# Cross-attention with layer norm on one core: when the next weights are turned, and which engine turns the later context

## The chip, the cores and the metric

The kernel runs on one core of a Trainium2 chip. A core has five engines that run side by side, each with its own queue of instructions: TensorE (matrix products and transposes), VectorE, ScalarE, GpSimd and SyncE, which here only issues DMA transfers. In the profile they are called PE (with PEld for the loading of weights), DVE, ACT, POOL and SP. An engine executes its queue in order, and an instruction waits until what it needs has been signalled by another engine or by a DMA that has landed. The metric is the device time of one execution in microseconds (us).

## What is computed

There are 16 batches of 256 queries of width 256, and 16 contexts of 77 keys of width 192. With 8 heads of width 256 the reference is, in short:

```python
Q = (img_embed @ Wq).reshape(B, -1, H, D).transpose(0, 2, 1, 3)
K = (sent_embed @ Wk).reshape(B, -1, H, D).transpose(0, 2, 1, 3)
V = (sent_embed @ Wv).reshape(B, -1, H, D).transpose(0, 2, 1, 3)
score = jnp.einsum('bhqd,bhkd->bhqk', Q, K) / math.sqrt(D)
mask = (atten_mask != 0)[:, None, None, :]
score = jnp.where(mask, score, -jnp.inf)
attn = jax.nn.softmax(score, axis=-1)
ctx = jnp.einsum('bhqk,bhkd->bqhd', attn, V).reshape(B, -1, H * D)
out = ctx @ Wo + img_embed
mu = jnp.mean(out, axis=-1, keepdims=True)
var = jnp.var(out, axis=-1, keepdims=True)
return (out - mu) * jax.lax.rsqrt(var + EPS) * gamma + beta
```

All values are 32-bit floats.

## The kernel before

The kernel never forms Q, K and V. For each head it multiplies the weights first: G = Wk Wq^T / 16 for the scores and U = Wv Wo for the output. Then A = G context^T (called `pa` in PSUM, `a` in SBUF) stands for a batch's keys, and the scores of a tile of 128 queries are x^T against A. The order of every engine's instructions is written out by hand: the kernel runs under a manual schedule, so the queues hold what the Python code issues, in that order.

The context width of 192 is split into 128 rows (`cA`) and 64 rows (`cB`; these are stored twice, in both halves of the partitions, so that two products can run side by side). G and U are split in the same way into `gA`, `gB` and `uA`, `uB`. The 77 keys are split into 64 and 13; the last 13 keys of all batches are gathered in `cRA` and `cRB`, and their product with U is `pr`, formed once by `prepare_last`.

The setup stage (until about 58 us of the profile) runs like this:

- SyncE issues the loads: the rows of Wk and Wq for the first head pairs (`wk_nat`, `wk_last`, `wq_nat`, L567 to L571), the first 336 rows of the context (`c_sb`, L564), then Wk and Wq for the other heads in blocks of 32 rows (`wk_blk`, `wq_blk`, L561), the other 896 rows of the context (`c_sb` again), Wv in blocks (`wvT`), Wo (`wo`, L590), the mask (`bias`, L591) and x in blocks (`xT`, L168). Later follow x in rows (`xg`, L144), gamma and beta. Each transfer counts on one of eight semaphores in turn, and it is issued only after the eighth transfer before it has landed.
- TensorE transposes the first weights through PSUM (`turn_k`, `turn_q`, L615; an identity matrix is the other operand), and ScalarE and VectorE in turn copy the results out (`evacuate`, L151 and L153). TensorE forms `pg` (L719, copied to `gA` by ScalarE, L726) and `ph` (L733, to `gB` by VectorE, L740). Then `turn_c(0, first)` transposes the first context rows on TensorE (`pc`, L653), with copies to `cA` and `cB` and a GpSimd copy of `cB` into the other half (L664).
- `a_of_places((0, 1))` forms the first half of A for the first group of four batches: 64 products with `cA` (`pa`, L199), 64 with `cB` (L213), and eight copies. The weights in blocks need no TensorE: `turn_blk` (L642) has VectorE transpose them in blocks of 32x32, and the following products (`pgb` L676, `phb` L690) contract over the blocks. `turn_blk(0)` stands before this call, `turn_blk(1)` among its copies, after the fourth.
- After `pgb` and `phb`, VectorE turns `wvT` (`turn_v`, L668), the second half of A is formed, and `turn_c(first, NCR)` transposes the remaining eight chunks of 112 context rows: 16 transposes on TensorE, four copies each on ScalarE, VectorE and GpSimd. GpSimd then gathers `cRA` and `cRB` (L782, L783), clears `vr` (L784) and turns the mask into a bias (L788).
- TensorE forms U (`pu` L676, then `pw` L690). ScalarE and VectorE copy it to `uA` and `uB`, and GpSimd copies `uB` to the other half (L807). `pr` follows (L274 with `cRA` and `uA`, L284 with `cRB` and `uB`), then the main loop.

The main loop runs over the 16 batches: scores (`ps`, L313), bias and maximum on VectorE (L328, L335), exponential on ScalarE (L342), normalising on GpSimd (L356), the turn of the weights on VectorE (L366), the products with the values (L429, L378), and the layer norm. PSUM has eight banks, from which all these results are taken in turn.

Of the kernel before, what the change touches and what calls it, by code (L numbers as in the profile page):

```python
# [8 lines left out]
F32 = mybir.dt.float32  # L9
# [6 lines left out]
P = 128  # L16
H = 8
D = 256
EPS = 1e-05
GB = 4  # L20
KM = 64
# [32 lines left out]
def kernel(  # L54
# [13 lines left out]
    nc = tc.nc  # L68
    B, S, DI = x.shape
    S2, DL = c.shape[1], c.shape[2]  # L70
    LB = DL - P
    CR = 112
    NCR = B * S2 // CR
    NG = B // GB
    QT = S // P
    NT = B * QT
# [3 lines left out]
    BK = 32  # L80
    NM = P // BK
    NL = DL // BK
    PW = (NF + 1) * BK
    assert KM == 2 * BK and NM == NF and 2 * KR <= BK
    assert NCR * CR == B * S2 and NG * GB == B and DI == 2 * P and D == 2 * P and 2 * LB == P


    engines = mybir.EngineType
# [25 lines left out]
    def of_e(u, e):  # L114
        return u[:, 3 - 2 * e : 5 - 2 * e].rearrange("p q n i c -> p (q n) i c")


    cA = const.tile([P, B, S2], F32, tag="cA", name="cA")
    cB = const.tile([P, B, S2], F32, tag="cB", name="cB")
    cRA = const.tile([P, B, KR], F32, tag="cRA", name="cRA")  # L120
    cRB = const.tile([P, B, KR], F32, tag="cRB", name="cRB")
# [12 lines left out]
    c_rows = c.rearrange("b k l -> (b k) l").rearrange("(r p) l -> p r l", p=CR)  # L134

    def flat(ap):
        return ap.rearrange("p a b -> p (a b)")
# [10 lines left out]
    def evacuate(dst, src):  # L148
        evacs[0] += 1
        if evacs[0] % 2:  # L150
            nc.scalar.copy(dst, src)  # L151
        else:
            nc.vector.tensor_copy(dst, src)  # L153
# [386 lines left out]
    early = ctx.enter_context(tc.tile_pool(name="early", bufs=1))  # L540
    pools[0] = turned = early
    with tc.tile_pool(name="wonce", bufs=1) as wp:
        c_sb = wp.tile([CR, NCR, DL], F32, tag="c", name="c_sb")


        wq_nat = wp.tile([P, 2, 2, 2 * D], F32, tag="w128", name="wq_nat")
# [12 lines left out]
        def load_blocks(to, blocks):  # L559
            for i in range(NM):  # L560
                nc.sync.dma_start(to[i * BK : (i + 1) * BK], blocks[i])  # L561

        def load_c(lo, hi):
            nc.sync.dma_start(c_sb[:, lo:hi, :], c_rows[:, lo:hi, :])  # L564

        first = -(-GB * S2 // CR)
        nc.sync.dma_start(wk_nat[:, 0], wk_rows[0][:, : 2 * D])  # L567
        nc.sync.dma_start(wk_last, wk_ends[:, : 2 * D])
        nc.sync.dma_start(wq_nat[:, 0], wq_rows[0][:, :, : 2 * D])
        nc.sync.dma_start(wk_nat[:, 1], wk_rows[1][:, : 2 * D])  # L570
        nc.sync.dma_start(wq_nat[:, 1], wq_rows[1][:, :, : 2 * D])  # L571
        load_c(0, first)
        for e in range(2):
            load_blocks(wk_blk[:, e], wk_blocks[2 * e + 1])
            load_blocks(wq_blk[:, e], wq_blocks[2 * e + 1])
        load_c(first, NCR)

        warm = const.tile([P, 1], F32, tag="warm", name="warm")
        nc.scalar.activation(warm, eps, AF.Exp)
# [8 lines left out]
            load_blocks(wvT[:, a], wv_blocks[a])  # L588
        for a in range(NF):
            nc.sync.dma_start(wo_of[a // 2][:, a % 2], wo_rows[a])  # L590
        nc.sync.dma_start(  # L591
            bias_f.bitcast(I32), mask.rearrange("b k -> (b k)").partition_broadcast(P)
        )
# [17 lines left out]
        def turn_chunks(of, name):  # L611

            pt = ps_mm.tile([P, 4, P], F32, tag="mm", name=f"pt_{name}")
            for i, chunk in enumerate(of):
                nc.tensor.transpose(pt[:, i], chunk, ident)  # L615
            return pt

        def turn_q(e, u):
            chunks = [
                wq_nat[:, e, t, u * D + dc * P : u * D + (dc + 1) * P]  # L620
                for dc in range(2) for t in range(2)
            ]
            pt = turn_chunks(chunks, f"q_{e}_{u}")
            evacuate(flat(qT[:, e, u]), flat(pt))

        def turn_k(e):
            pt = turn_chunks([wk_nat[:, e, n * P : (n + 1) * P] for n in range(4)], f"k_{e}")
            evacuate(
                kT[:, e].rearrange("p u n l -> p (u n) l")[:, :, :P], pt
            )  # L630
# [9 lines left out]
        def turn_blk(e):  # L640
            for blk, of in ((wk_blk, kT_blk), (wq_blk, qT_blk)):
                nc.vector.transpose(  # L642
                    of[:, e].rearrange("p n (m r) -> p m n r", r=BK),
                    blk[:, e].rearrange("p m (n c) -> p m n c", c=BK),
                )

        def turn_c(lo, hi):
            for r in range(lo, hi, 2):
                n = min(2, hi - r)
                pc = ps_mm.tile([P, 4, P], F32, tag="mm", name=f"pc_{r}")  # L650
                for lc in range(2):
                    for j in range(n):
                        nc.tensor.transpose(  # L653
                            pc[:, 2 * lc + j, :CR],
                            c_sb[:, r + j, lc * LB : lc * LB + P],
                            ident[:CR, :CR],
                        )
                rows = slice(r * CR, (r + n) * CR)
                evacuate(flat(cA)[:, rows].rearrange("p (j m) -> p j m", m=CR), pc[:, :n, :CR])
                evacuate(  # L660
                    flat(cB)[LB:, rows].rearrange("p (j m) -> p j m", m=CR),
                    pc[LB:, 2 : 2 + n, :CR],
                )
                nc.gpsimd.tensor_copy(flat(cB)[:LB, rows], flat(cB)[LB:, rows])  # L664

        def turn_v(a):
            blocks = wvT[:, a].rearrange("p m (c n) -> p m n c", n=4)
            nc.vector.transpose(blocks, blocks)  # L668
# [3 lines left out]
        def of_pair(out, a, weight, moving):  # L672

            for n in range(4):
                for e in range(2):
                    nc.tensor.matmul(  # L676
                        out[e][:, a % 2, :],
                        weight(a, e, n)[:, :P],
                        moving(a, e, n),
                        start=(n == 0),  # L680
                        stop=(n == 3),
                    )
# [16 lines left out]
        def two_banks(name, j):  # L699
            return [ps_mm.tile([P, 2, DI], F32, tag="mm", name=f"{name}_{j}_{e}") for e in range(2)]  # L700
# [13 lines left out]
        def g_of(e):  # L714

            pg = ps_mm.tile([P, 2, DI], F32, tag="mm", name=f"pg_{e}")
            for u in range(2):
                for dc in range(2):
                    nc.tensor.matmul(  # L719
                        pg[:, u],  # L720
                        kT[:, e, u, dc, :P],
                        qT[:, e, u, dc],
                        start=(dc == 0),
                        stop=(dc == 1),
                    )
            nc.scalar.mul(gA[:, NF * e : NF * e + 2], pg, D ** -0.5)  # L726

        def rest_of_g(u):

            ph = ps_mm.tile([P, DI], F32, tag="mm", name=f"ph_{u}")  # L730
            for dc in range(2):
                for e in range(2):
                    nc.tensor.matmul(  # L733
                        ph[half(e)],
                        kT[:, e, u, dc, P:],
                        qT[:, e, u, dc],
                        start=(dc == 0),
                        stop=(dc == 1),
                    )
            nc.vector.tensor_scalar(gB[:, u], ph, D ** -0.5, None, ALU.mult)  # L740

        def a_of_places(places, between=None):
            part_A, part_B, copies = prepare_a(0, places)
            part_A()
            part_B()
            for i, (dst, src) in enumerate(copies()):
                evacuate(dst, src)
                if between and i == 3:
                    between()

        turn_k(0)
        keep_busy(2)
# [1 line left out]
        keep_busy(3)  # L754
        turn_q(0, 0)
        turn_q(0, 1)
        g_of(0)
        turn_k(1)
        turn_q(1, 0)
        turn_q(1, 1)  # L760
        g_of(1)
        rest_of_g(0)
        rest_of_g(1)
        turn_c(0, first)
        turn_blk(0)
        a_of_places((0, 1), lambda: turn_blk(1))
        pg = two_banks("pgb", 0)
        for e in range(2):
            of_pair(pg, e, wk_part, wq_part)
# [8 lines left out]
        nc.sync.dma_start(bet, beta.partition_broadcast(P))  # L778
        a_of_places((2, 3))
        turn_v(3)  # L780
        turn_c(first, NCR)
        nc.gpsimd.tensor_copy(cRA, cA[:, :, KM:])  # L782
        nc.gpsimd.tensor_copy(cRB, cB[:, :, KM:])  # L783
        nc.gpsimd.memset(vr, 0.0)  # L784


# [3 lines left out]
        for j in range(NF // 2):  # L790
            pu = two_banks("pu", j)
            for a in range(2 * j, 2 * j + 2):
                of_pair(pu, a, wv_part, wo_part)
            for e in range(2):
                evacuate(
                    of_e(uA, e)[:, :, 2 * j : 2 * j + 2].rearrange("p n a c -> p a n c"),
                    pu[e].rearrange("p a (n c) -> p a n c", c=BK),
                )
# [32 lines left out]
    for b in range(-1, B - 1):  # L831
# [9 lines left out]
        g, n = (b + 1) // GB + 1, (b + 1) % GB  # L841
# [107 lines left out]
```

## Time and profile before

| what | value |
|---|---|
| time, median of 3 runs | 283.19 us (283.01 to 283.97) |
| the profiled execution, its own time | 282.59 us |
| its span, first to last instruction | 280.8 us |
| mean granted TensorE clock | 0.991 |
| TensorE busy | 270.8 us (96%) |
| VectorE busy | 206.1 us (73%) |
| GpSimd busy | 168.2 us (60%) |
| ScalarE busy | 166.5 us (59%) |

The page of the profile gives busy times in 40 equal slices of about 7 us, in tenths:

```profile
PE   7899999999999999999999999999999999999990
DVE  0255762668748989888889787777797978788873
ACT  2312142148547767676767676767686866968751
POOL 1000049955677777786867878777778445426173
DMA  6998898940000010960100109501001011010112
```

The first eight slices are the setup. There the DMA engines are busy almost throughout, and afterwards they are mostly idle. In the views below, a line of a timeline or of the chain starts with the start and the duration in us, then engine, line of code and instruction. Matmul ends are modelled, so the starts of the next instruction are the safer numbers. Times are compared with times of executions, spans with spans; what lies between (1.8 us here) is outside the first and last instruction.

### The profile page before, as it was taken

Reading aid. Unit: us, or ns where it says so; the run is one execution under the profiler, and the core shown is the slowest. Engines: PE = TensorE matmul, PEld = TensorE weight load, DVE = VectorE, ACT = ScalarE, POOL = GpSimd, SP = SyncE. Lnnn points to the kernel's source line nnn. Section 1 sums busy time; section 2 is a strip of 40 time slices with the busy share of each in tenths; the row PEclk is TensorE's granted clock in tenths of the full one; section 3 lists DMA queues with packets and bytes.
Section 4 is the critical chain, followed back from the end, with each engine's and each line's share of the span. In section 5 each row is a group of like instructions: output and inputs, shape, how many; then the busy total and the mean of one; then the engine's idle time right before and its main releaser. Section 6 shows DMA issues by size and latency. Waiting matters only on the chain.

```text
span 280.8 us, 13274 instructions
## 1 busy us (share of the span) xinstructions
PE 270.8 (96%) x5925; PEld 195.6 (70%) x5925; DVE 206.1 (73%) x421; ACT 166.5 (59%) x447; POOL 168.2 (60%) x228
## 2 busy tenths in 40 slices
PE   7899999999999999999999999999999999999990
PEld 7756589985586868686868686868686868476550
DVE  0255762668748989888889787777797978788873
ACT  2312142148547767676767676767686866968751
POOL 1000049955677777786867878777778445426173
PEclk9999999999999999999999999999999999999996
DMA  6998898940000010960100109501001011010112
GB/s 191 246 230 176 279 267 227 166 139 4 2 6 2 5 40 2 191 189 5 42 3 5 40 5 198 180 8 38 7 2 42 2 42 38 4 41 2 40 37 78
DMA packets 35641, 22.61 MB, mean 81 GB/s; under 512 B 17712, under 2 KB 34048, under 8 KB 35584
## 3 DMA queue, kind: packets, MB, share of 16 engines
q1 hardware_dynamic: 35584, 21.77, 30.8%
q8 instruction: 46, 0.75, 1.2%
q14 instruction: 11, 0.09, 0.1%
HBM read 17.57 MB, written 4.19 MB: 77 GB/s over the span
## 4 chain that ended last, share of the span: by engine, by line
PE 89%; POOL 2%; ACT 2%; DMA 2%; DVE 2%; issue 0%; SPq 0%; ACTq 0%; POOLq 0%
PE ps L313 23%; PE pa L199 12%; PE pv L241 9%; PE po L429 9%; PE pm L429 7%; PE pa L213 6%; PE pv L252 5%; PE po L378 5%; PE pu L676 3%; PE pr L274 2%; DMA wq_nat<-in_L_xattn_Wq_dram 2%; ACT e L342 1%; PE pg L719 1%; PE pgb L676 1%; PE pw L690 1%; PE pr L284 1%
## 5 line engine op out<-in xcount | busy, mean ns | idle before, releaser
L342 ACT ACTIVATE e<-s,top 128x77 f32<-128x77 f32 x256 | 67.1, 346 | 52.1 <-DVE top L335 49.9
L356 POOL TENSOR_TENSOR p<-e,rden 128x512 f32<-128x512 f32 x64 | 45.8, 738 | 46.6 <-DVE rden L350 46.4
L313 PE MATMUL ps<-a,xT 128*32 128x154 f32 x2048 | 70.0, 294 | 0.0
L313 PEld LDWEIGHTS ps<-a,xT 128*32 128x32 f32 x2048 | 66.2, 110 | 1.6 <-issue 0.7
L328 DVE TENSOR_TENSOR s<-ps,bias 128x308 f32<-128x308 f32 x64 | 30.3, 475 | 17.6 <-PE ps L313 15.9
L199 PE MATMUL pa<-cA,gA 128*32 128x308 f32 x512 | 35.8, 423 | 0.4 <-ACT cA L151 0.4
L462 POOL TENSOR_TENSOR xg<-xg,m 128x256 f32<-128x256 f32 x33 | 24.2, 733 | 13.5 <-DVE xg L476 11.8
L199 PEld LDWEIGHTS pa<-cA,gA 128*32 128x32 f32 x512 | 16.4, 110 | 21.1 <-issue 7.6
L241 PE MATMUL pv<-uA,cA 128*32 128x512 f32 x256 | 30.4, 592 | 0.0
L366 DVE STREAM_TRANSPOSE pT<-p 128x640 f32<-128x640 f32 x32 | 25.6, 824 | 2.4 <-POOL p L356 2.4
L348 DVE TENSOR_REDUCE den<-e 128x8 f32<-128x616 f32 x32 | 24.7, 772 | 3.5 <-ACT e L342 3.5
L335 DVE TENSOR_REDUCE top<-s 128x8 f32<-128x616 f32 x32 | 25.4, 795 | 1.1
L664 POOL COPY cB<-cB 64x224 f32<-64x224 f32 (+1 forms) x6 | 1.9, 358 | 36.8 <-DVE cB L153 36.8
L392 POOL TENSOR_TENSOR ts<-vw 128x768 f32<-128x768 f32 x11 | 22.0, 1997 | 0.0
L213 PE MATMUL pa<-cB,gB 64*32 64x308 f32 x512 | 19.5, 420 | 0.0
L378 PE MATMUL po<-vw,pT 128*32 128x256 f32 x320 | 19.2, 380 | 0.0
L861 ACT COPY vw<-pv 128x512 f32<-128x512 f32 x32 | 16.9, 578 | 2.5 <-PE pv L252 2.5
L495 ACT ACT_TABLE_LOAD x14 | 18.0, 1283 | 0.3
L213 PEld LDWEIGHTS pa<-cB,gB 64*32 64x32 f32 x512 | 9.7, 107 | 11.3 <-issue 7.6
L252 PE MATMUL pv<-uB,cB 64*32 64x512 f32 x256 | 17.4, 601 | 0.0
L524 DVE SCALAR_TENSOR_TENSOR xg<-xg,mv,gam 128x256 f32<-128x256 f32 x25 | 17.1, 682 | 0.0
L861 ACT COPY a<-pa 128x308 f32<-128x308 f32 x48 | 16.6, 446 | 0.0
(114 smaller groups left out, 440.1 us busy)
## 6 DMA issues: line engine op xcount, KB each, us to landing
xT<-in_x_dram SPq DMA_DIRECT2D x16, 256.0 KB, 6.4
xg<-in_x_dram SPq DMA_DIRECT2D x4, 1024.0 KB, 8.0
out_dram<-xg SPq DMA_DIRECT2D x15, 256.0 KB, 2.3
wo<-in_L_xattn_Wo_dram SPq DMA_DIRECT2D x4, 512.0 KB, 5.3
wvT<-in_L_xattn_Wv_dram SPq DMA_DIRECT2D x16, 96.0 KB, 3.7
wq_nat<-in_L_xattn_Wq_dram SPq DMA_DIRECT2D x2, 512.0 KB, 6.7
wq_blk<-in_L_xattn_Wq_dram SPq DMA_DIRECT2D x8, 128.0 KB, 4.3
wk_blk<-in_L_xattn_Wk_dram SPq DMA_DIRECT2D x8, 96.0 KB, 6.1
```

Of the source, the lines that this page charges most:

```text
L199: nc.tensor.matmul(flat(o[i * BK : (i + 1) * BK]), gA[:, h, cols(dc, i)], flat(cA[:, batches, :]), start=not B_first, stop=B_first,)
L213: nc.tensor.matmul(flat(banks[j + k][i * BK : (i + 1) * BK]), gB[half(k), h % NF, cols(dc, i)], flat(cB[half(k), batches, :]), start=B_fir ...
L241: nc.tensor.matmul(pv[k][i * BK : (i + 1) * BK], cA[:, b, k * BK : (k + 1) * BK], uA[:, parts, :, i], start=True, stop=False,)
L252: nc.tensor.matmul(pv[k][i * BK : (i + 1) * BK], cB[half(k), b, k * BK : (k + 1) * BK], uB[half(k), parts, :, i], start=False, stop=True,)
L313: nc.tensor.matmul(ps[m // 2][i * BK : (i + 1) * BK, m % 2 * 2 * S2 : (m % 2 + 1) * 2 * S2], xT_of[g][:, j * NM + m, dc], flat(a_of[g][:, ...
L328: nc.vector.tensor_tensor(s[:, a * H // 2 : (a + 1) * H // 2], ps[a][:, : H // 2 * S2].rearrange("p (h k) -> p h k", k=S2), bias[:, b, :]. ...
L342: nc.scalar.activation(e[:, h], s[:, h], AF.Exp, bias=top[:, h : h + 1])
L356: nc.gpsimd.tensor_tensor(part, e_mh[:, :, :, keys], rden_mh.unsqueeze(3).to_broadcast(list(part.shape)), ALU.mult,)
L366: nc.vector.transpose(pT_of[t].rearrange("p n m q -> p m n q"), p.rearrange("p m (n k) -> p m n k", k=BK),)
L378: nc.tensor.matmul(po[i * BK : (i + 1) * BK], pT[:, n, i], vw_of[b][:, 2 - n // 2 * 2 : 4 - n // 2 * 2, n % 2, :] if n < NF else vr[:, b, ...
L429: nc.tensor.matmul(out[i * BK : (i + 1) * BK], weight[:, i], moving, start=(n == 0), stop=(n == len(terms) - 1),)
L861: nc.scalar.copy(dst, src)
```

## The change

Four things change.

First, the order of the setup on TensorE: `turn_k(1)` goes ahead of `g_of(0)`, and `turn_c` (for the first context rows) ahead of `g_of(1)`. Second, `turn_blk(1)` goes ahead of `a_of_places((0, 1))` instead of between its copies. Third, the context rows beyond the first 336 are no longer loaded as rows and turned by TensorE. They are loaded in 32x32 blocks straight into `cA` and `cB`, by six DMAs (four for `cA`, two for the upper half of `cB`) behind Wo and ahead of the mask. `turn_rest` then has VectorE turn the blocks in place and GpSimd make the copies. Fourth, `turn_rest` is called in the second pass of the loop that forms `pu`, so its two VectorE transposes stand between the two `uA` copies of VectorE, and its GpSimd copies stand behind the clearing of `vr` and the bias. `c_sb` shrinks to three chunks.

```diff
+        first = -(-GB * S2 // CR)
+        c_sb = wp.tile([CR, first, DL], F32, tag="c", name="c_sb")
...
+        rest = slice(first * CR, None)
+        assert (B * S2 - first * CR) % BK == 0
+
+        def load_rest():
+
+            blocks = c.rearrange("b k l -> (b k) l")[rest].rearrange("(m r) l -> r m l", r=BK)
+            for l in range(NL):
+                i, of = (l, cA) if l < NM else (l - NM + LB // BK, cB)
+                nc.sync.dma_start(
+                    flat(of)[i * BK : (i + 1) * BK, rest].rearrange("p (m q) -> p m q", q=BK),
+                    blocks[:, :, l * BK : (l + 1) * BK],
+                )
+
+        def turn_rest():
+            nc.vector.transpose(flat(cA)[:, rest], flat(cA)[:, rest])
+            nc.gpsimd.tensor_copy(cRA, cA[:, :, KM:])
+            nc.vector.transpose(flat(cB)[LB:, rest], flat(cB)[LB:, rest])
+            nc.gpsimd.tensor_copy(flat(cB)[:LB, rest], flat(cB)[LB:, rest])
+            nc.gpsimd.tensor_copy(cRB, cB[:, :, KM:])
+
...
-        load_c(0, first)
+        nc.sync.dma_start(c_sb, c_rows[:, :first, :])
...
-        load_c(first, NCR)
...
+        load_rest()
         nc.sync.dma_start(
             bias_f.bitcast(I32), mask.rearrange("b k -> (b k)").partition_broadcast(P)
         )
...
         turn_q(0, 0)
         turn_q(0, 1)
+        turn_k(1)
         g_of(0)
-        turn_k(1)
         turn_q(1, 0)
         turn_q(1, 1)
+        turn_c()
         g_of(1)
         rest_of_g(0)
         rest_of_g(1)
-        turn_c(0, first)
         turn_blk(0)
-        a_of_places((0, 1), lambda: turn_blk(1))
+        turn_blk(1)
+        a_of_places((0, 1))
...
         a_of_places((2, 3))
         turn_v(3)
-        turn_c(first, NCR)
-        nc.gpsimd.tensor_copy(cRA, cA[:, :, KM:])
-        nc.gpsimd.tensor_copy(cRB, cB[:, :, KM:])
         nc.gpsimd.memset(vr, 0.0)
...
             for a in range(2 * j, 2 * j + 2):
                 of_pair(pu, a, wv_part, wo_part)
+            if j:
+                turn_rest()
             for e in range(2):
                 evacuate(
```

## What was predicted

> **What bounds the kernel now.** I read the page's chain of work that ended last, then the same chain in order of time over the first 60 us, then the timelines of the engines, and the DMA share last. TensorE is 89% of the chain and is never idle from 17.27 us to the tail at 260. Whatever TensorE is spared before 58 us therefore comes off the end, as long as nothing it needs comes late.
>
> ```profile
> PE 89%; POOL 2%; ACT 2%; DMA 2%; DVE 2%; issue 0%; SPq 0%; ACTq 0%; POOLq 0%
> ```
>
> The chain in order of time (start, us, what) shows where the change acts:
>
> ```profile
> 7.23 0.67 PE pt_q L615 x4
> 7.90 0.02 issue
> 7.92 0.70 DVE qT L153
> 8.62 0.14 issue
> 8.76 1.97 PE pg L719 x8
> 10.72 0.44 PE pt_k L615 x4
> 11.16 0.45 PE pt_q L615 x4
> 11.61 0.02 issue
> 11.63 0.59 ACT qT L151
> 12.23 0.04 issue
> 12.27 1.99 PE pg L719 x8
> 14.27 1.88 PE ph L733 x16
> 16.14 0.55 PE pc L653 x4
> 16.69 0.02 issue
> 16.71 0.51 ACT cA L151 x2
> 17.22 0.04 issue
> 17.27 4.35 PE pa L199 x64
> ...
> 36.15 1.69 PE pc L653 x16
> ```
>
> The reader should see three places where TensorE hands over to a copy (VectorE at 7.92, ScalarE at 11.63 and 16.71) and waits for it, and 1.69 us of TensorE transposes of the context at 36.15. The TensorE timeline puts those idle times at 0.44, 0.24 and 0.40 us. Next I read what else is near the limit. On GpSimd's timeline (start, us, instruction):
>
> ```profile
> 40.80 3.51 POOL L784 MEMSET vr<- 128x4096 f32 x1
> 44.40 4.38 POOL L788 TENSOR_SCALAR bias<-bias 128x1232 f32<-128x1232 int32 x1
> 48.84 3.57 POOL L807 COPY uB<-uB 64x256 f32<-64x256 f32 x8
> ```
>
> GpSimd works without a pause from 38.79 to 60.5. The sixth of the eight uB copies ends at 51.51, and TensorE's pr group on uB (L284) loads its first weights around 52. That is 0.5 us of slack, the smallest in this stage. The bias operation needs the mask, which SyncE issues at 30.95 and which lands 9.2 us later, at 40.2. It was ready in time.
>
> **What the Trainium skill says.** "SBUF — State Buffer", section "Door 1: The DMA port swizzle", says that a transfer into 32 partitions reaches 8 of the 16 ports, and gives 189 GB/s at 1 MiB. The trace agrees: the xT loads (32 partitions, 256-byte runs, 256 KB each) follow each other at 1.35 us, 194 GB/s. "DMA: Bandwidth & Descriptors", section "Why small descriptors are slow", counts 32-byte beats plus about 3 cycles a packet, so 11 for 256 bytes and 7 for 128. No 128-byte packet of data is in this trace. "VectorE: DVE Perf Modes", section "The three transpose paths", has VectorE turn 32x32 blocks only, into SBUF. The trace prices that: kT_blk 128x768 takes 0.97 us, qT_blk 128x1024 takes 1.20.
>
> **The change part by part, on the profiled execution** (span 280.8 us, 1.8 outside it, 282.59 in all; the median of three runs is 283.19, so I take the difference and subtract it from that).
>
> 1. Order at the start. The built order of TensorE becomes pt_q, pt_q, pt_k(1), pg(0), pt_q, pt_q, pc x6, pg(1), ph, ph, pa.
>  - pt_k(1) needs its wk rows, which SyncE issues at 2.10 and which land 6.5 us later, at 8.56. TensorE is free at about 8.3, so it waits a quarter us, runs 0.44, and pg(0) starts at 9.05 instead of 8.76.
>  - pg(0) takes 1.96, to 11.01. The two pt_q (0.45 each) run to 11.91. The first context rows (issued at 3.08, 8.6 us to landing) are there at 11.7, so six pc transposes of 0.096 each run to 12.5.
>  - pg(1) wants the qT copy of ScalarE. That engine copies gA from 11.03 to 11.63 and then qT to 12.22, so it is done. pg(1) runs 12.55 to 14.55 and ph to 16.42.
>  - pa starts at 16.43 instead of 17.27: its cA copies ended near 13.1, and gA's second copy (0.60) ends at 15.2. Gain 0.84. This equals the three idle times, 1.08, less the new wait of about 0.25.
> 2. turn_blk(1) goes ahead of A's copies on VectorE. The last wq block (issued at 15.74, 4.3 us to landing) is there at 20.04. VectorE does gB until 16.9, then turns 0.97, 1.20, 0.97, and the last (1.20) from 20.1 to 21.3. Queued behind it are the A copies, wanted at 22.43 less 0.84, or 21.6. It fits by 0.3 us. If it did not, ScalarE's banks come first: in the built order the next four groups of TensorE wait for ScalarE's copies. Cost 0.
> 3. The 16 pc transposes at 36.15 go: gain 1.69. pu then starts at 35.3. Its wvT and wo come earlier than before, since 672 KB of context rows no longer stand ahead of them (about 2.9 us at the 222 GB/s of 20 to 23 us). Its banks need one A copy of each engine, done at 34.4 and 34.6. The eight evacuations of pc go too (ScalarE 1.50, VectorE 1.32), off the path. Sum of 1 and 3: 2.53 us.
> 4. turn_rest on VectorE, between the uA copies (41.95 and 45.69 before, 2.5 earlier after). It transposes 128x896 and 64x896, by the row of 128x768 about 1.1 us each, from 40.1 to 42.4, and the next uA copy is wanted at 43.2. Hidden, if the context has landed by about 41.
> 5. GpSimd. The memset of vr (3.51) moves ahead of everything and falls into its idle time after 18 us. Four cB copies (1.33) go, and one of 64x896 comes (about 1.0, the memset's 0.86 ns an element and a start). In the new order bias stands first, then cRA (0.31), cB (1.0), cRB (0.31), uB.
> 6. SyncE's queue. Six DMAs of 112 KB with 896 packets of 128 bytes stand between wo and the mask, replacing one of 672 KB further ahead. The mask, xT of group 0, xg, gamma, beta and xT of group 1 are issued behind them. Only the mask is near its use: xT landed at 46.6 and was turned from 51.9, and xg is used after 80.
>  - Price of the six: at the port rate of 194 GB/s 3.5 us (lower end); by 7/11 of a 256-byte packet's 21 ns, 4.5; at a full 21 ns a packet (56 per DMA and engine), 7.1 (upper end). I take 5.2.
>  - The mask: 40.2, less 2.9 for the rows gone from ahead, less what is won back of the idle DMA time, plus 5.2. The windows have the DMA share at 0.53 from 25 to 30 us, 2.35 us idle; each load is issued only when the eighth load before it has landed, and SyncE's waits show 3.5 us on the landing of context rows. I take 1.8 of it as won. The mask lands at 40.7, with 38.8 to 43.5 as its ends.
>
> ```profile
> 25.00:30.00 5.00, 5.00 (x64) 3.76 (x67) 1.50 (x4) 1.08 (x2) 0.00 (x0) 1.00 0.53 146
> ```
>
> (The last two numbers are DMA share and GB/s.) What the mask may take: TensorE will want the sixth uB copy at 49.5 (52.0 less 2.5). GpSimd needs 4.43 for bias, 1.62 for the three copies, 2.68 for six uB copies, and 0.1 for signals: 8.8 us. The limit is 40.6; a mask at 40.7 costs 0.1, and each us later costs one. cRA, for the first pr group, has its limit at 41.7, so it comes second. I put 0.2 us on this. Expected gain 2.53 - 0.2 = 2.3 us; 283.19 - 2.3 = 280.9.
>
> **The rivals.**
> - R1, the late mask, partly: it lands between 41.3 and 42.3, and 0.7 to 1.7 us of the gain becomes a wait of TensorE before pr. For it: the limit has no slack, and no packet of this size has been seen. Against: VectorE's and GpSimd's work are both shorter, and the DMA queue has idle time to give. Time: 283.19 - 2.5 + 1.2 = 281.9.
> - R2, the other side: the packets of 128 bytes cost more than any row shows, so that the mask lands after 43.1 (40.6 + 2.5), where the wait eats the whole gain. The place is TensorE between pw and pr. It decides slower from 44.0, that is from 8.5 us for the six DMAs. At twice my price, 10.4 us, the mask lands at 45.9: 283.19 - 2.5 + 5.3 = 286.0. For it: such packets start on odd 128-byte places half the time, and 512-byte blocks of wvT already moved at only about 200 GB/s. Against: 256-byte packets lose nothing to 512-byte ones here.
> - R3, the start gives nothing: the context rows or wk land later than in this one execution, or VectorE's turn waits for its blocks and holds the A copies. Then only the 1.69 stays: 281.5. Against: the loads ahead of these are untouched.
> - R4, the tail: 2.5 us won early are lost to a later engine. Against: from 58 to 260 us the chain is TensorE alone, and GpSimd's last bias step moves 2.5 us with it.
>
> **How the numbers follow.** Chances: forecast 0.56; R1 0.16; R3 and R4 together 0.10; mask near 43.1, no change, 0.08; R2 0.10. A measurement of this kernel tells about 0.3%, 0.85 us, from no change. Faster takes the forecast, R1 and R3 with R4: 0.82; same 0.08; slower 0.10. The range runs from 280.2 (all of 2.53, and 0.4 more where the mask is early and the start has no new wait) to 283.2 (mask at 43.1); R2 and half of the no-change case lie outside, less than 2 in 10. The likeliest case's own range is 280.2 to 281.4.
>
> **What would show it.** In the trace after: pa from about 16.4; no pc near 36; pu from 35.3; pr's first group from 46.8; scores from 55.8 instead of 58.3; span near 278.5. The mask's landing, the start of the bias operation on GpSimd and TensorE's idle time before L284 decide between the forecast, R1 and R2. An idle time of TensorE before pg(1) or at pgb would show step 1 or 2 wrong. TensorE waiting for cRA or uA before pr, or VectorE waiting for DMA at turn_rest, would show step 4 or 6 mis-sized.

## The result and the profile after

The change makes no difference that can be measured.

| | before | after |
|---|---|---|
| median time, 21 runs each | 282.76 us (282.11 to 283.97) | 282.84 us (281.76 to 286.19) |
| ratio to before, 95% interval | | 1.001 [0.9996, 1.0024] |
| profiled execution, its time and span | 282.59, 280.8 us | 282.9, 281.1 us |
| start of the scores (`ps`), first batch | 58.25 us | 57.83 us |
| start of the scores, last batch | 257.68 us | 258.31 us |

One run of the kernel after, the one of 286.19 us, had a lower clock (0.981, where the others had 0.986 to 0.997) and is left out of the ratio.

The forecast was 280.9 us, faster. The work at the start did become shorter, as predicted, but the two last rows say that most of it is gone by the first scores, and that the main loop then loses more than what is left. I read the same views again. First, the chain of work that ended last, its share by engine (SPq is SyncE's queue):

```profile
PE 74%; SPq 10%; DMA 6%; POOL 4%; ACT 2%; DVE 1%; issue 1%; ACTq 0%; POOLq 0%
```

TensorE had 89% of the chain before. Now the issuing of loads, the transfers and GpSimd stand in it with 20%. TensorE's timeline of the kernel after (start, us, engine, line, instruction, and in brackets the idle time before it and what ended it):

```profile
16.45 4.35 PE L198 MATMUL pa<-cA,gA 128*32 128x308 f32 x64
...
35.03 7.85 PE L693 MATMUL pu<-wo,wvT 64*128 64x256 f32 x64
42.81 3.75 PE L707 MATMUL pw<-wo,wvT 64*64 64x256 f32 x64
47.66 3.08 PE L273 MATMUL pr<-cRA,uA 128*128 128x208 f32 x16 [1.10 <-POOL cRA L579]
51.80 3.08 PE L283 MATMUL pr<-cRB,uB 64*128 64x208 f32 x32 [1.06 <-POOL uB L822]
...
57.83 4.39 PE L312 MATMUL ps<-a,xT 128*32 128x154 f32 x128
```

The same two places in the kernel before:

```profile
37.77 7.84 PE L676 MATMUL pu<-wo,wvT 64*128 64x256 f32 x64
...
58.25 4.39 PE L313 MATMUL ps<-a,xT 128*32 128x154 f32 x128
```

`pa` begins at 16.45 us and `pu` at 35.03, where it was 37.77 before: 2.7 us won. Then TensorE stands still twice for GpSimd, 2.2 us in all. GpSimd's timeline of the kernel after shows why it is late:

```profile
14.20 3.51 POOL L797 MEMSET vr<- 128x4096 f32 x1
42.91 4.38 POOL L801 TENSOR_SCALAR bias<-bias 128x1232 f32<-128x1232 int32 x1 [25.19 <-DMA bias<-in_mask_BxS_if_dram]
47.25 0.36 POOL L579 COPY cRA<-cA 128x208 f32<-128x208 f32 x1
47.67 0.93 POOL L581 COPY cB<-cB 64x896 f32<-64x896 f32 x1
48.66 0.36 POOL L582 COPY cRB<-cB 128x208 f32<-128x208 f32 x1
49.08 3.58 POOL L822 COPY uB<-uB 64x256 f32<-64x256 f32 x8
```

GpSimd idles for 25.19 us until the mask lands, at 42.75 by its semaphore, and everything that TensorE wants of it is queued behind the bias operation. SyncE's queue in the kernel after shows what the mask waited for (SPq durations are the time that issuing takes, a blocked queue included):

```profile
16.29 9.54 SPq L561 DMA_DIRECT2D wvT<-in_L_xattn_Wv_dram  x16
25.88 1.86 SPq L606 DMA_DIRECT2D wo<-in_L_xattn_Wo_dram  x4
27.79 6.88 SPq L572 DMA_DIRECT2D cA<-in_ctx_dram  x4
34.71 2.27 SPq L572 DMA_DIRECT2D cB<-in_ctx_dram  x2
37.03 0.54 SPq L608 DMA_DIRECT2D bias<-in_mask_BxS_if_dram  x1
```

The six context loads keep SyncE for 9.2 us (one of them alone for 4.02), so the mask is not issued before 37.03 us. In the kernel before it was issued at 30.95:

```profile
30.95 0.70 SPq L591 DMA_DIRECT2D bias<-in_mask_BxS_if_dram  x1
```

Meanwhile the DMA engines are not full, as the stretches of the kernel after say (the last two numbers are the DMA share and GB/s):

```profile
20.00:25.00 5.00, 5.00 (x98) 3.09 (x88) 3.02 (x5) 1.68 (x4) 0.00 (x0) 1.00 0.74 207
25.00:30.00 5.00, 5.00 (x72) 3.10 (x72) 1.36 (x3) 1.08 (x2) 0.00 (x0) 1.00 0.78 217
...
35.00:40.00 5.00, 5.00 (x50) 4.97 (x44) 2.97 (x5) 1.10 (x3) 0.00 (x0) 1.00 0.77 139
```

The second loss is in the main loop. The chain in order of time (start, us, what), up to the scores of the sixth batch, in the kernel after:

```profile
120.54 1.89 PE pm L428 x64
122.42 1.30 PE po L428 x45
123.72 0.63 issue
124.35 1.17 PE po L428 x34
125.52 4.20 PE ps L312 x126
```

In the middle of 80 products `po`, after 45 records, TensorE does nothing for 0.63 us and waits for nothing that the profile shows. The scores of this batch start 14.93 us after those of the batch before, and the next ones 14.32 us later, where all around it is 14.10. That is 0.83 + 0.22 = 1.05 us. The kernel before has nothing of the kind there:

```profile
122.85 2.18 PE po L429 x80
125.03 4.19 PE ps L313 x128
```

The sum: 0.42 won before the loop, 1.05 lost in it, 0.63 later at the last scores. The span is only 0.3 longer, because what follows the last scores took 22.8 us instead of 23.1. All the kernels below that load the context in blocks have 22.8 or 22.9 there, and the one that does not has 23.1; why is not known.

### The profile page after: what moved, and what is told of

Read it like the earlier page. It is cut to its first block, busy times and chain, and to the rows that moved or that the text cites. A ratio compares the mean times of both kernels' runs of the same rounds, so it can differ in the third digit from the quotient of the medians.

```text
span 281.1 us, 13245 instructions
## 1 busy us (share of the span) xinstructions
PE 269.2 (96%) x5909; PEld 194.8 (69%) x5909; DVE 207.0 (74%) x419; ACT 165.0 (59%) x443; POOL 168.0 (60%) x225
## 4 chain that ended last, share of the span: by engine, by line
PE 74%; SPq 10%; DMA 6%; POOL 4%; ACT 2%; DVE 1%; issue 1%; ACTq 0%; POOLq 0%
PE ps L312 23%; PE pv L240 9%; PE pa L198 9%; PE po L428 9%; PE pm L428 7%; PE pv L251 5%; PE po L377 5%; PE pa L212 4%; SPq L561 3%; SPq L572 3%; DMA wq_nat<-in_L_xattn_Wq_dram 3%; DMA xT<-in_x_dram 2%; SPq L167 2%; DMA wq_blk<-in_L_xattn_Wq_dram 2%; ACT e L341 1%
## 5 line engine op out<-in xcount | busy, mean ns | idle before, releaser
L198 PEld LDWEIGHTS pa<-cA,gA 128*32 128x32 f32 x512 | 17.5, 110 | 19.9 <-issue 7.1
L801 POOL TENSOR_SCALAR bias<-bias 128x1232 f32<-128x1232 int32 x1 | 4.4, 4385 | 25.2 <-DMA bias<-in_mask_BxS_if_dram 25.2
L428 PE MATMUL po<-vr,pT 128*32 128x128 f32 x352 | 16.2, 273 | 0.6 <-issue 0.6
## 6 DMA issues: line engine op xcount, KB each, us to landing
wq_blk<-in_L_xattn_Wq_dram SPq DMA_DIRECT2D x8, 128.0 KB, 4.0
```

What stands on the lines that cost most here:

```text
L198: nc.tensor.matmul(flat(o[i * BK : (i + 1) * BK]), gA[:, h, cols(dc, i)], flat(cA[:, batches, :]), start=not B_first, stop=B_first,)
L428: nc.tensor.matmul(out[i * BK : (i + 1) * BK], weight[:, i], moving, start=(n == 0), stop=(n == len(terms) - 1),)
```

## The experiments

Two things had to be explained. Theory A for the setup: the mask is late because six loads of 128-byte packets stand ahead of it, and this late mask takes what the change wins. Its rivals are that the new place of GpSimd's and VectorE's work costs the time whatever the mask does, or that the start's new order gives nothing. For the main loop, the theory is that the pause depends on where in TensorE's instruction stream a place of the loop lies: the change takes 16 transposes (5925 matmul records before, 5909 after, and as many weight loads) from the stream. Its rival is that something the loop works on comes late. All ratios are to the kernel before, run on the same chip in the same rounds.

**The mask ahead of the six loads** (the changed kernel with one call moved).

```diff
-        load_rest()
         nc.sync.dma_start(
             bias_f.bitcast(I32), mask.rearrange("b k -> (b k)").partition_broadcast(P)
         )
+        load_rest()
```

> The changed kernel with one edit: the mask is issued ahead of the six context loads instead of behind them. Theory (the late mask is the whole loss): the mask lands about 37 instead of 42.75, the bias operation ends by 41.5, the two waits of TensorE at pr (1.10 and 1.06 us) go, scores start at about 55.8, and the time is 2.5 us under the kernel before, about 280.3 (ratio 0.991). Rival (the wait only moves): the six context loads now land 1.6 us later, VectorE waits for them at its two transposes, uA and cRA come late, and TensorE still waits 1 us or more before pr: ratio 0.995 or more. Rival (the start-up stage does not matter): as the changed kernel, ratio 1.00.

Measured: 280.10 us, ratio 0.9909 [0.9895, 0.9922]. The mask landed at 38.78, later than the 37 that were expected. GpSimd's timeline of this kernel:

```profile
38.94 4.38 POOL L801 TENSOR_SCALAR bias<-bias 128x1232 f32<-128x1232 int32 x1 [21.46 <-DMA bias<-in_mask_BxS_if_dram]
43.28 0.36 POOL L579 COPY cRA<-cA 128x208 f32<-128x208 f32 x1
45.53 0.93 POOL L581 COPY cB<-cB 64x896 f32<-64x896 f32 x1 [1.89 <-DVE cB L580]
```

and TensorE's:

```profile
46.25 3.08 PE L273 MATMUL pr<-cRA,uA 128*128 128x208 f32 x16
49.66 3.08 PE L283 MATMUL pr<-cRB,uB 64*128 64x208 f32 x32 [0.33 <-POOL uB L822]
52.68 3.08 PE L273 MATMUL pr<-cRA,uA 128*128 128x208 f32 x16
55.69 4.39 PE L312 MATMUL ps<-a,xT 128*32 128x154 f32 x128
```

The bias operation starts 4.0 us earlier, the wait for `cRA` is gone and the one for `uB` is 0.33. The scores start at 55.69, where the prediction had 55.8. Now the context is what comes late: VectorE waits 1.61 us for `cA` and 1.91 for `cB`, and GpSimd 1.89 for VectorE. That costs TensorE only the 0.33. Moving one call gives back 2.7 us of time, so Theory A holds for its first half: the mask's place in the queue is what took the gain, and the new work on GpSimd and VectorE is not. The pause in the loop is still there, at 121.58 us, after the same 45 products, though all of this happens 2.1 us earlier than in the changed kernel.

**Only the new order of the start** (the kernel before, with these lines of the change and nothing else).

```diff
+        turn_k(1)
         g_of(0)
-        turn_k(1)
...
+        turn_c(0, first)
         g_of(1)
...
-        turn_c(0, first)
         turn_blk(0)
-        a_of_places((0, 1), lambda: turn_blk(1))
+        turn_blk(1)
+        a_of_places((0, 1))
```

> The kernel before with only the order of the setup changed (turn_k(1), the first turn_c and turn_blk(1) moved as in the change); the later context stays loaded in rows and turned by TensorE. Theory: pa starts at 16.45 instead of 17.27, GpSimd's work moves with it and the mask (40.2) is there before GpSimd asks for it (about 43.6), so 0.8 us come off the end: 282.0, ratio 0.997. Rival (VectorE's earlier turn_blk(1) holds the A copies, or the start gains nothing at the end): ratio 1.000 or above.

Measured: 281.63 us, ratio 0.9964 [0.9952, 0.9976]. TensorE in this kernel:

```profile
36.57 7.85 PE L676 MATMUL pu<-wo,wvT 64*128 64x256 f32 x64
...
57.06 4.39 PE L313 MATMUL ps<-a,xT 128*32 128x154 f32 x128
```

The order alone moves `pu` from 37.77 to 36.57, and the 1.2 us arrive at the scores and at the end. GpSimd's bias operation starts at 43.20 behind the clearing of `vr`, with no wait for the mask, TensorE does not wait between `pu` and `pr`, and there is no pause near 123 us (this kernel has 5925 matmul records again; one interval of its scores, further on, is 14.29 us). So the start's new order is worth 1.2 us.

**Only the context in blocks** (the changed kernel with the old order of the start, the reverse of the lines above).

> The changed kernel with the order of the setup put back to that of before; the later context loads in blocks and is turned by VectorE. Theory (the end of the setup is fixed by the mask's landing): TensorE arrives at pr 0.8 us later than in the changed kernel and waits 0.8 us less there (about 1.3 instead of 2.16 in all), scores start at 57.8 as in the changed kernel, ratio 0.9985, within 0.1% of the changed kernel. Rival (each part gives its share by itself): 0.8 us slower than the changed kernel.

Measured: 283.35 us, ratio 1.0028 [1.0013, 1.0043]. That is slower than before, where a little faster was expected. `pu` starts at 36.24, 1.5 us earlier than before, but the mask lands at 42.43, `pr` waits for `uB` (0.70 us, where about 1.3 in all was expected), and the scores start at 57.50: 0.75 earlier, close to the theory. The rest of the miss is in the loop. Two pauses stand there, near 123.4 and 128.0 us, and the intervals of the scores are 14.66 and 14.87 us instead of 14.10, which costs 1.33. The last scores start at 258.25, 0.57 later than before, and the time is 0.5 longer. So the loss in the loop belongs to the blocks, not to the order.

**Sixteen idle transposes on TensorE** (the changed kernel, with as many matmuls as the kernel before).

```diff
         for j in range(0, GT, 2):
             transpose_x(0, j)
+        idle = ps_mm.tile([P, P], F32, tag="mm", name="idle_2")
+        keep_busy(16)
         prepare_last()
```

> The changed kernel with 16 idle transposes on TensorE just before pr, where it waits about 2.2 us anyway. They bring TensorE's instructions in the main loop back to the places in the program that they have in the kernel before. Theory (the 0.83 us gap of TensorE near 123 us and the 0.22 us in the next batch come from the loop's instructions standing elsewhere in the program, and are met by an instruction fetch): the gaps are gone, the loop runs at 14.10 us a batch throughout, scores still start near 57.8, and the time is about 1.0 us under the changed kernel (ratio to before 0.997 to 0.998). Rival (the gap comes from the loads of the third group, which run at that time): the gap stays and the time is that of the changed kernel.

Measured: 282.26 us, ratio 0.9977 [0.9965, 0.9989]. The chain of this kernel in order of time, at the place of the pause:

```profile
122.65 2.18 PE po L428 x80
124.83 1.17 PE ps L312 x35
```

The pause is gone, and the scores follow each other at 14.10 us throughout. They start at 58.06 in the first batch and at 257.48 in the last, 0.8 earlier than in the changed kernel. The median is 0.6 us under that of the changed kernel, and 0.8 when each is compared with the kernel before in its own rounds; 1.0 was expected. Nothing that the loop works on was changed, so the pause hangs on the places of the instructions. The wait for `uB` is still there (1.08 us), since the mask is as late as it was.

**The same six loads in long runs** (the changed kernel; it loads other context values, the same number of bytes as 32 contiguous runs of 3584 bytes for each load instead of 896 packets of 128).

```diff
-            blocks = c.rearrange("b k l -> (b k) l")[rest].rearrange("(m r) l -> r m l", r=BK)
+            runs = c.rearrange("b k l -> (b k l)")[first * CR * DL :].rearrange("(n r w) -> n r w", n=NL, r=BK)
...
+                nc.sync.dma_start(flat(of)[i * BK : (i + 1) * BK, rest], runs[l])
```

> The changed kernel with the six context loads fetching the same bytes into the same places as 32 contiguous runs of 3584 bytes each, so that other context values stand in the tiles; everything else is unchanged. Theory A (small packets delay the mask): the six take 3.5 us instead of 5.65, the mask lands near 40.5, TensorE waits under 0.3 us at pr, and the time is about 2.2 us under the kernel before (ratio 0.992). Theory B (the mask is late because SyncE issues the loads ahead of it late, whatever their packets): the mask lands within 0.7 us of 42.75 and the time is that of the changed kernel.

Measured: 280.49 us (279.78 to 283.30, 15 runs), ratio 0.9930 [0.9907, 0.9952], which is 2.3 us less than the changed kernel. But the execution that was profiled took 282.82 us, with the mask at 42.46 and waits of 1.59 and 1.08 us. Three more executions of the same kernel were profiled.

> The kernel with long context runs again, for a second profile: its first profile was of one of its longest executions (282.82, median 280.49), with the mask at 42.5. Theory A (small packets delay the mask): in an execution of about 280.3 the mask lands at 40.7 or before and TensorE waits under 0.3 us before pr. If the mask lands as late as 42.5 in an execution near 280.3, theory A falls.

> A third look at the kernel of e4 (the six loads as 32 runs of 3584 bytes each), to catch a profiled execution near 280.3 us. Theory A (the load of small packets holds the mask back): in an execution of 280.8 us or less the mask lands by 40.8, the bias operation starts by 41.0 and TensorE waits at most 0.3 us before pr, with the scores from 56.0 or earlier. Rival (the time is won in the main loop): the mask lands after 41.5 and the scores start after 56.6 as in both earlier profiles, and the main loop is shorter by over 1 us.

> The same kernel once more, for the same purpose. Theory A: in an execution of 280.8 us or less the mask lands by 40.8 and TensorE waits at most 0.3 us before pr. Rival: the mask lands after 41.5 and the main loop is shorter by over 1 us.

The three executions took 282.15, 280.68 and 282.32 us, with the bias operation at 41.91, 40.69 and 42.74. The second of them is one like the median. SyncE's queue in it:

```profile
27.80 2.01 SPq L572 DMA_DIRECT2D cA<-in_ctx_dram  x4
29.86 1.81 SPq L572 DMA_DIRECT2D cB<-in_ctx_dram  x2
32.68 0.35 SPq L605 DMA_DIRECT2D bias<-in_mask_BxS_if_dram  x1
```

and GpSimd and TensorE in it:

```profile
40.69 4.38 POOL L798 TENSOR_SCALAR bias<-bias 128x1232 f32<-128x1232 int32 x1 [23.04 <-DMA bias<-in_mask_BxS_if_dram]
```

```profile
49.58 3.08 PE L283 MATMUL pr<-cRB,uB 64*128 64x208 f32 x32
...
55.60 4.39 PE L312 MATMUL ps<-a,xT 128*32 128x154 f32 x128
```

Wo's last rows landed at 34.81 here and at 34.77 in the changed kernel, so the two can be compared from there on. The six loads then took 3.83 us in long runs and 4.93 in small packets: 1.1 us are the transfer itself. (The other three profiles of long runs had 3.61 to 3.86, the three other kernels with the small packets ahead of the mask 5.10 to 5.33.) The mask landed 1.88 us after them here, and 3.05 after them in the changed kernel. Here it was issued at 32.68, and its packets (the only ones of 4928 bytes) moved from 35.31 on, beside those of the six loads. There it was issued at 37.03, and its first packet moved at 38.59; from 36.0 to 37.1 us the DMA engines had been mostly idle (a share of 0.30). So the late issue fits the other 1.2 us. It is not shown for all of them: in two of the other profiles of long runs the mask was issued at 33.35 and 32.90, and yet landed 2.68 and 2.58 us after the six loads. Without both delays, the profile shows TensorE in no wait between `pu` and `pr`, and the scores start at 55.60. From landing to landing, 672 KB in 3.83 us are 180 GB/s. The Trainium skill ("SBUF — State Buffer", section "Door 1: The DMA port swizzle") gives 189 for transfers into 32 partitions at 1 MiB, which agrees roughly (the first packets of the six loads moved before Wo had landed).

The other three profiles of this kernel were late mainly for another reason: Wo's last rows landed at 35.55, 35.97 and 36.80. In the last of them Wo was issued at 27.56, 1.7 us later, because SyncE had been held longer by earlier loads; there the mask came at 42.58 and TensorE waited 0.56 and 1.06 us. With the mask this near its limit, the speed of the transfers in each execution decides, which fits the spread of the 15 runs. The rival named for the third profile, that the time is won in the loop, is out: the loop took 200.47 us here and 200.48 in the changed kernel.

**Half of Wv issued by GpSimd** (the changed kernel, the clearing of `vr` and eight of the sixteen `wvT` loads on GpSimd's queue, behind its two `cB` copies).

```diff
-        for a in range(NF):
+        for a in range(2):
             load_blocks(wvT[:, a], wv_blocks[a])
...
         turn_c()
+        nc.gpsimd.memset(vr, 0.0)
+        for a in range(2, NF):
+            load_blocks(wvT[:, a], wv_blocks[a], nc.gpsimd)
```

> The changed kernel with half of the wvT loads (8 of 16) issued from GpSimd's queue behind its clearing of vr, instead of all from SyncE. Theory A (SyncE's issue of 0.485 us a load holds back wo, the context blocks and the mask, while the DMA engines have idle time): wo, the context blocks and the mask land at least 1.5 us earlier than in the changed kernel (mask 41.2 or before), the waits before pr shrink to 0.6 us or less, time about 281.2, ratio 0.994. Theory B (the DMA engines themselves set the time of the mask): mask within 0.5 us of 42.75, ratio 1.00.

Measured: 281.35 us, ratio 0.9946 [0.9926, 0.9966]. SyncE's queue in this kernel:

```profile
20.95 2.21 SPq L606 DMA_DIRECT2D wo<-in_L_xattn_Wo_dram  x4
23.62 11.01 SPq L572 DMA_DIRECT2D cA<-in_ctx_dram  x4
34.67 1.13 SPq L572 DMA_DIRECT2D cB<-in_ctx_dram  x2
35.84 0.54 SPq L608 DMA_DIRECT2D bias<-in_mask_BxS_if_dram  x1
```

Wo is issued 4.9 us earlier. This is what the Trainium skill advises where the making of descriptors is the limit ("Perfetto Trace Analysis", section "DMA Optimizations": spread the transfers over the engines that can issue them). The trace agrees only in part. The DMA engines are now full from 20 to 30 us (shares of 1.07 and 1.02 in the two stretches that had 0.74 and 0.78). But Wo's last rows land at 34.01, only 0.76 us earlier than in the changed kernel, the six loads at 39.14, 0.56 earlier, and the mask at 41.42, 1.33 earlier, since the four `cA` loads now hold SyncE for 11 us. At least 1.5 was expected of all three. The wait for `cRA` is gone, the one for `uB` is 1.08 us (at most 0.6 was expected), and the scores start at 56.53, 1.30 earlier. The time was as expected, but partly by luck: 0.54 us more came from the loop, where the pause was shorter this time (0.08 us, in intervals of 14.38 and 14.32).

One more thing can be read here. The third `cA` load let go of SyncE's queue at 33.08 us, 0.39 after Wo's third load had landed. In the changed kernel it did so at 33.36, 0.38 after that landing, and in the two other kernels with the six loads ahead of the mask 0.37 and 0.40 after it. So it looks as if the queue were held until the loads ahead have moved, and not by the issuing alone; that would explain why an earlier issue of Wo helps so little. No run tests this by itself.

**The mask first, and other places in TensorE's stream** (the kernel of the first experiment, with 16 narrow products, 32 matmul records in the trace, added before the first `turn_q`).

```diff
+        for i in range(16):
+            nc.tensor.matmul(idle[:32, :32], ident[:, :32], ident[:, :32], start=True, stop=True)
         turn_q(0, 0)
```

> The kernel with the mask ahead of the context loads, and 16 narrow products (32 columns) on TensorE early, where it waits for the first Wq rows. Theory (instruction places): the gap near 121 us goes; the fillers cost less than 0.5 us; time 279.3 to 279.8, ratio 0.987 to 0.989. Rival (the gap is not set by the places): 280.1 or above, ratio 0.991 or more.

Measured: 279.63 us (279.39 to 280.31), ratio 0.9888 [0.9869, 0.9907]; the lowest median of all versions, though its interval overlaps that of the first experiment. The mask landed at 36.27, and nothing stops TensorE before `pr`; the scores start at 55.67. The pause near 121 us is gone. A smaller one stands at another place of the chain of this kernel:

```profile
176.67 2.16 PE po L428 x74
178.83 0.21 issue
```

Here the scores are 14.49 and 14.31 us apart, 0.60 lost. The pause can be moved and made smaller by instructions that do nothing; this one still has it.

The loop of all the profiled kernels, by the number of matmul records in TensorE's stream:

| matmul records | kernel | first to last scores, us |
|---|---|---|
| 5925 | before | 199.43 |
| 5925 | order only | 199.61 |
| 5925 | 16 idle transposes | 199.42 |
| 5909 | changed | 200.48 |
| 5909 | mask first | 200.45 |
| 5909 | blocks only | 200.75 |
| 5909 | long runs, four profiles | 200.67, 200.77, 200.47, 200.09 |
| 5909 | half of Wv from GpSimd | 199.94 |
| 5941 | mask first, 16 narrow products | 200.03 |

## Why the prediction was wrong

- **Step 1** was right: `pa` at 16.45 us, predicted 16.43. The new waits are there too (0.47 us for the Wk rows, predicted a quarter, and 0.30 for the context rows).
- **Step 2** was right: VectorE's blocks were done at 21.1, the A copies then waited 0.52 us for TensorE and not the other way round, and `pgb` began at 22.97 without a wait.
- **Step 3** was right: `pu` at 35.03, predicted 35.3. The experiments split it: the order alone moved `pu` by 1.20 us (predicted 0.84), the blocks alone by 1.53 (predicted 1.69 for the transposes; in that profile `pa` began 0.39 later than before, after a longer wait for the first Wq rows, so single profiles differ by this much).
- **Steps 4 and 5** were right in size: VectorE's two transposes took 1.10 and 1.11 us (predicted 1.1 each), GpSimd's copy of 64x896 took 0.93 (predicted 1.0), and the clearing of `vr` went into idle time.
- **Step 6** failed, in the term "I take 1.8 of it as won": 1.8 us of idle DMA time that the mask should have won back. The sum had 40.2 - 2.9 - 1.8 + 5.2 = 40.7. The price of the six loads was about right (4.93 us). The rows gone from ahead and the idle time together brought Wo's last landing from 38.09 to 34.77, 3.3 us where the sum had 4.7. With 2.9 for the rows, only 0.4 of the idle time was won. Then the mask took 3.05 us behind the last load ahead of it, where it had taken 2.1 before (40.2 less 38.1), so 0.9 was lost that the sum did not have. The measured sum is 40.2 - 2.9 - 0.4 + 4.9 + 0.9 = 42.7. Part of the reason lies in SyncE. Its 16 `wvT` loads go out at 0.60 us each, waits included, so Wo was not issued before 25.88, and the six loads keep the queue until 37.03. I had counted the six loads as bytes and packets on the DMA engines, but not as time in the queue that issues them, though the mask is behind them there too. That the six loads ahead of the mask are what makes it late is shown by moving it (first experiment); how much of that is their bytes and how much their time in the queue is not. For Wo the queue is only a part, since an issue 4.9 us earlier made it land 0.76 earlier; why so little of the idle time was won stays open.
- **Two readings** in step 6 were off without changing this. 672 KB at 222 GB/s are 3.1 us, not 2.9, which leaves 0.2 for the idle time. And in the trace before, the `xT` loads of a group land 1.14 to 2.88 us apart, 1.55 in the median, not 1.35; that is 169 GB/s and not 194, so the lower end of the price was too low.
- **The limit** of the mask, on the other hand, was right: 40.6 us for `uB`, or 40.3 with `pu` 0.3 earlier. A mask at 42.75 should then cost 2.4 us. From `pu` to the scores 22.80 us passed, where 20.48 had passed before: 2.3. And in the execution with the mask at 40.52, 0.2 past the limit, the second `pr` group began 3.17 us after the first, where 3.01 is the least. So the mechanism is that of R1, the late mask, with more of it than R1 had, just short of R2's point of 43.1. That the measured time came out at no change, the prediction's case for a mask at 43.1, is owed to the pause as well.
- **What no case had** is the pause in the loop, 1.05 us. The argument against R4 was that from 58 us on the chain is TensorE alone, so that what is won early stays won. It holds for waits on other engines, but not for a change of TensorE's own instruction stream. With the pause taken out by 16 idle transposes, the median was 282.26, between R1's 281.9 and no change.

Together: 2.7 won at `pu`, 2.3 lost to the mask, 1.05 to the pause, 0.3 won after the last scores. In the profiled execution that is 0.3 slower, in the medians nothing.

What stays open is why the pause falls where it does, but the traces go some way. In the changed kernel a packet on the queue of instructions (q8 in the profile) starts at 122.1 us, shortly before the pause, while the output and the next rows of x load the DMA engines. In the kernel before and with 16 transposes added, the packets there start at 119.6 and 118.6, 3.8 and 4.6 us ahead of TensorE's record of the same number. What the changed kernel shows holds for all the pauses: nine of the profiles have one and two of them a second, and in all eleven TensorE goes on 2.2 to 2.5 us after the start of a packet on q8. Counted in TensorE's records, matmuls and weight loads together, the eleven lie at 4545, 4801 and 7617, give or take one, so they are whole multiples of 256 records apart; and q8 has 46 packets of 16 KB for some 11,870 records, or 258 for each. So an instruction fetch that comes too late is very likely. But no run took the traffic away or moved a fetch by itself, so why the packet starts late is not shown. The runs show that the pause comes and goes with the instructions before it.

## What to carry to other kernels

A load put ahead of another can cost that one twice: its bytes on the DMA engines, and the time for which it holds the queue that issues both; ask of each small, urgent transfer what is issued ahead of it, and put it first. Idle DMA time in a profile is not simply there for the taking: the queue that issues may be what leaves it idle, and filling it may still not bring forward the load that matters. And where TensorE is busy to the end, removing its instructions can shift a pause into a loop far behind: compare the intervals between equal places of the loop before and after, and try a few idle instructions.

## What the runs showed of the hardware

- A load of 896 packets of 128 bytes held SyncE's queue for 4.02 us in the changed kernel and for 7.94 with half of Wv on GpSimd's queue, and four of them for up to 11.0; the same bytes in 32 runs of 3584 bytes held it for 0.3 to 0.7 us each.
- Six loads of 112 KB into 32 partitions each took 4.93 to 5.33 us in packets of 128 bytes (four kernels) and 3.6 to 3.9 us in runs of 3584 bytes (four profiles), counted from Wo's last landing.
- Eight loads of `wvT` occupied GpSimd for 4.71 us, 0.59 each, when GpSimd issued them.
- TensorE can pause for 0.1 to 0.8 us without waiting for any engine, and with what follows it this cost 0.5 to 1.3 us of a loop of 200. The eleven pauses end 2.2 to 2.5 us after a packet on the queue of instructions starts, and lie multiples of 256 TensorE records apart. Sixteen idle transposes, 1.8 us of work put where TensorE waited anyway, made the kernel 0.6 to 0.8 us faster.
